# Experts on their own tokens: rows scattered to slots of one expert and gathered back, in a two-layer graph network with a mixture of experts

## The chip, the cores and the metric

The kernel runs on one core of a Trainium2 chip. The core has a matrix engine (PE, with its weight loads shown as PEld), a vector engine (DVE), a scalar engine (ACT), a general engine (POOL, which can also issue DMAs) and a synchronisation engine (SP, which here only issues DMAs). Each engine runs its own instructions in the order in which the built program has them. The metric is the device time of one execution in microseconds, as the median of several runs.

## The reference, cut to what matters

The input is 64 batches of 256 tokens of 256 features, all float32. A dense graph layer, a dense layer, a second graph layer and a mixture of eight experts follow each other, each on the normalised tokens and each added to its input.

```python
x = x + gnn0(layernorm(x), adj, W0, a0)      # 4 heads, softmax over masked scores, elu
x = x + layernorm(x) @ weight.T + bias
x = x + gnn1(layernorm(x), adj, W1, a1)      # 1 head, relu
x = x + moe(layernorm(x))

def moe(tokens):                             # 16384 tokens of 256
    logits = tokens @ router_w.T             # 8 experts
    rw, re = top_k(softmax(logits), 2)
    rw = rw / rw.sum(-1)
    combine = zeros(N, 8).at[arange(N)[:, None], re].set(rw)
    out = tokens
    for e in range(8):
        h = gelu(tokens @ w1[e] + b1[e])
        out = out + combine[:, e:e+1] * (h @ w2[e] + b2[e])
    return out
```

Each token keeps two experts of eight; the loop above computes all eight and weights six of them with zero.

## The kernel before, in words

The kernel is written against a tiling layer: the program is traced in Python, and a scheduler then fixes each engine's order, taking work in the order in which it was traced wherever its inputs and buffers let it. Tiles of one tag rotate through a fixed number of buffers, so an instruction can wait for a buffer as well as for data.

The work goes by pairs of batches: 32 pairs, each of 512 tokens, which are four tiles of 128 rows. `batch_layers` is a generator that does both graph layers and the dense layer for one batch; `layers` lets the two batches of a pair take turns. In one batch, `project` normalises (L159 to L166, with two small POOL operations at L162 and L163), transposes on PE (L176), copies the transposed tokens out of PSUM on ACT (L179) and multiplies with the layer's weights (L190). `attention` makes the scores z per head (L209 to L223), transposes them (L234), copies (L238) and multiplies with q (L241). Four heads in the first graph layer, one in the second. At the end the normalised tokens are transposed into xT (L179 again), and POOL writes base, the sum that the experts add to (L294).

After both batches, `layers` computes the router's logits (L308), ranks the experts and gives weights comb that are zero for six experts (L313 to L334), and adds the second biases (L345, L347).

`experts` then runs each of the eight experts on all 512 tokens of a pair: four products of 512 columns into ph (L357), two gelus (L361), eight products of 256 columns into py (L367) and four weighted additions into base (L373). All expert weights lie on the chip for the whole kernel; POOL loads them at the start (L144 to L150).

The last loop takes one step of the next pair's layers between each two experts of a pair, so the experts of pair p lie beside the layers of pair p+1. SP loads one pair's tokens per step (L66) and stores one pair's result.

Of the kernel before, what the change touches and what calls it, by code (L numbers as in the profile page):

```python
# [8 lines left out]
F32 = mybir.dt.float32  # L9
AF = mybir.ActivationFunctionType  # L10
ALU = mybir.AluOpType
AX = mybir.AxisListType

P = 128


def rows_to_all(ap: bass.AP, n: int) -> bass.AP:
    """A contiguous vector of n elements in DRAM, read into every partition."""
    return bass.AP(tensor=ap.tensor, offset=ap.offset, ap=[[0, P], [1, n]])
# [3 lines left out]
def kernel(  # L23
# [27 lines left out]
    EPS = 1e-5  # L51
    SLOPE0, SLOPE1 = 0.2, 0.01
# [5 lines left out]
    small = ctx.enter_context(tc.tile_pool(name="small", bufs=4))  # L58
    psum = ctx.enter_context(tc.tile_pool(name="psum", bufs=2, space=bass.MemoryType.PSUM))
# [19 lines left out]
    # before[e, f] = 1 where expert f comes before expert e: ties go to the lower index.  # L79
    before = const.tile([P, E, E], F32, tag="before", name="before")  # L80
    nc.vector.memset(before, 0.0)
    for e in range(1, E):
        nc.vector.memset(before[:, e, :e], 1.0)

    adj_i = const.tile([P, NT, N], adj.dtype, tag="adj_i", name="adj_i")
    nc.sync.dma_start(out=adj_i, in_=adj.rearrange("(t p) j -> p t j", p=P))
    # Added to the scores before the leaky ReLU, which brings a masked one to the reference's fill.
# [9 lines left out]
    def gnn_weights(w, a, heads, name):  # L97
        """[W | W a_src | W a_dst], so one product gives q and both score terms."""
# [41 lines left out]
    w1s = const.tile([P, E, KT, D], F32, tag="w1s", name="w1s")  # L140
    w2s = const.tile([P, E, KT, D], F32, tag="w2s", name="w2s")
    b1s = const.tile([P, E, KT], F32, tag="b1s", name="b1s")
    b2s = const.tile([E, D], F32, tag="b2s", name="b2s")
    nc.gpsimd.dma_start(out=b2s, in_=b2)  # L144
    nc.gpsimd.dma_start(out=b1s, in_=b1.rearrange("e (t p) -> p e t", p=P))
    for e in range(0, E, 2):
        nc.gpsimd.dma_start(
            out=w1s[:, e : e + 2], in_=w1[e : e + 2].rearrange("e (k p) f -> p e k f", p=P)
        )
        nc.gpsimd.dma_start(  # L150
            out=w2s[:, e : e + 2], in_=w2[e : e + 2].rearrange("e (k p) f -> p e k f", p=P)
        )

# [1 line left out]
    def layernorm(src):  # L155
# [8 lines left out]
        xn = work.tile([P, NT, D], F32, tag="xn", name="xn")  # L164
# [16 lines left out]
    def project(src, wx, heads):  # L181
        """q of one batch, with both score terms in its last columns."""
# [14 lines left out]
    def attention(q, heads, mask, slope):  # L197
        """Per head: exp(scores - row max), its row sums, and its product with q, in PSUM.

        Yields between the two, and returns the values and 1 / sums.  # L200
        """
# [48 lines left out]
    def batch_layers(p, i, xT, base):  # L250
        """Both graph layers and the dense layer for one batch, in steps."""
# [40 lines left out]
        xn = layernorm(x2)  # L292
        transpose_tokens(xn, xT[:, :, i * N : (i + 1) * N])
        nc.gpsimd.tensor_add(base[:, i * NT : (i + 1) * NT, :], x2, xn)  # L294

    def layers(p):
        """Every layer before the experts for two batches, in steps; the batches take turns."""
        xT = io.tile([P, KT, TOK], F32, tag="xT", name=f"xT_{p}", bufs=3)
        base = io.tile([P, TT, D], F32, tag="base", name=f"base_{p}", bufs=3)
        steps = [batch_layers(p, i, xT, base) for i in range(2)]  # L300
        while steps:
            steps = [g for g in steps if next(g, steps) is not steps]
            yield

        pl = psum.tile([P, TT, E], F32, tag="mm", name="pl")
        for t in range(TT):
            for k in range(KT):
                nc.tensor.matmul(  # L308
                    pl[:, t, :], xT[:, k, t * P : (t + 1) * P], rT[:, k, :],
                    start=(k == 0), stop=(k == KT - 1),  # L310
                )
        lg = small.tile([P, TT, E], F32, tag="lg", name="lg")
        nc.vector.tensor_copy(lg, pl)  # L313
        lmax = small.tile([P, TT], F32, tag="lmax", name="lmax")
        nc.vector.tensor_reduce(lmax, lg, AX.X, ALU.max)
        comb = io.tile([P, TT, E], F32, tag="comb", name=f"comb_{p}", bufs=3)
        nc.vector.tensor_sub(comb, lg, lmax[:, :, None].to_broadcast([P, TT, E]))
        nc.scalar.activation(comb, comb, AF.Exp)
        # How many experts stand ahead of each: a greater logit, or an equal one at a lower index.
        ahead = small.tile([P, TT, E, E], F32, tag="ahead", name="ahead", bufs=1)  # L320
        tie = small.tile([P, TT, E, E], F32, tag="tie", name="tie", bufs=1)
        other = lg[:, :, None, :].to_broadcast([P, TT, E, E])
        own = lg[:, :, :, None].to_broadcast([P, TT, E, E])
        nc.vector.tensor_tensor(ahead, other, own, ALU.is_gt)
        nc.vector.tensor_tensor(tie, other, own, ALU.is_equal)
        nc.vector.tensor_mul(tie, tie, before[:, None, :, :].to_broadcast([P, TT, E, E]))
        nc.vector.tensor_add(ahead, ahead, tie)
        rank = small.tile([P, TT, E], F32, tag="rank", name="rank")
        nc.vector.tensor_reduce(rank, ahead, AX.X, ALU.add)
        nc.vector.scalar_tensor_tensor(comb, rank, 1.5, comb, op0=ALU.is_lt, op1=ALU.mult)  # L330
        tot = small.tile([P, TT], F32, tag="tot", name="tot")
        nc.vector.tensor_reduce(tot, comb, AX.X, ALU.add)
        nc.vector.reciprocal(tot, tot)
        nc.vector.tensor_mul(comb, comb, tot[:, :, None].to_broadcast([P, TT, E]))  # L334

        # The experts' second biases, weighted: comb @ b2.
        pc = psum.tile([E, TT, P], F32, tag="tr", name="pc")
        for t in range(TT):
            nc.tensor.transpose(pc[:, t, :], comb[:, t, :], ident)
        combT = small.tile([E, TT, P], F32, tag="combT", name="combT", bufs=1)  # L340
        nc.vector.tensor_copy(combT, pc)
        for i in range(2):
            pb = psum.tile([P, NT, D], F32, tag="mm", name="pb")
            for t in range(NT):
                nc.tensor.matmul(pb[:, t, :], combT[:, i * NT + t, :], b2s, start=True, stop=True)  # L345
            half = base[:, i * NT : (i + 1) * NT, :]
            nc.vector.tensor_add(half, pb, half)  # L347
        return xT, base, comb

    def experts(p, xT, base, comb):  # L350
        """Every expert on two batches, weighted into base; a step an expert."""
        for e in range(E):
# [82 lines left out]
```

## Time and profile before

| | |
|---|---|
| median of 3 runs | 3353.58 us (3351.46 to 3354.95) |
| span of the profiled execution | 3349.4 us; the page gives no other time for it, so 2 to 6 us of a run lie outside the span |
| instructions | 38810 |
| DVE busy | 1906.8 us (57%) |
| ACT busy | 1695.9 us (51%), of it 436 table loads of 1.283 us |
| POOL busy | 520.8 us (16%) |
| DMA | 41.76 MB, mean 12 GB/s |
| HBM | 22.50 MB read, 16.78 MB written |
| chain of waits, by engine | PE 62%, DVE 22%, ACT 7%, POOL 5%, issue 3% |

The profile page has the busy time of each engine, the span in 40 slices, the chain of work that ended last, and the costliest groups of instructions. A group's row gives its line, engine, operation, tiles and count, then the total busy time, the mean of one instruction in ns, and the engine's idle time just ahead of it with what ended that. The view by windows gives each engine's busy time in a stretch with the clock that PE was granted (PEclk, 1.00 is full), the mean busy share of the 16 DMA engines and the GB/s moved. The view in order of time gives start, duration, engine, line and tiles; rows of SPq are DMA issues on SP.

### The profile page before, as it was taken

The page shows a single profiled execution, that of the slowest core. Times are in us where ns is not written, and L with a number is a line of the kernel's source. Part 1 is how long each engine was busy: PE and PEld are TensorE (multiplying, and loading weights), DVE is VectorE, ACT ScalarE, POOL GpSimd, SP SyncE. Part 2 cuts the span into 40 slices and gives each one's busy share as a digit, 9 for nine tenths or more (in the row PEclk, how much of TensorE's full clock was granted, in tenths as well). Part 3 has the DMA queues.
Part 4 walks back from the last instruction along what each step waited for, and adds up shares of the span by engine and source line. Part 5 has one row for each costly group of instructions (what it writes and reads, how often), then busy time and mean ns, then how long its engine had stood idle before and what let it go on. Part 6 is the DMA issues. An engine that isn't in the chain of part 4 may idle for free.

```text
span 3349.4 us, 38810 instructions
## 1 busy us (share of the span) xinstructions
PE 3101.1 (93%) x14086; PEld 2180.6 (65%) x14086; DVE 1906.8 (57%) x4927; ACT 1695.9 (51%) x3156; POOL 520.8 (16%) x720
## 2 busy tenths in 40 slices
PE   5899999999999999999999999999999999999999
PEld 4566666666666666666666666666666666666666
DVE  5555656556565556565565655565655656555653
ACT  2444555545555445555455554455554555544552
POOL 2111101111111111011111111110111111111100
PEclk7899999999999999999999999999999999999999
DMA  2000000000000000000000000000000000000000
GB/s 88 1 13 13 7 13 13 7 13 13 7 13 7 13 13 7 13 13 7 13 13 7 13 7 13 13 7 13 13 7 13 13 7 13 7 13 13 1 7 13
DMA packets 36750, 41.76 MB, mean 12 GB/s; under 512 B 1344, under 2 KB 35408, under 8 KB 36560
## 3 DMA queue, kind: packets, MB, share of 16 engines
q1 hardware_dynamic: 35328, 35.07, 3.4%
q0 software_dynamic: 1232, 4.21, 0.4%
q8 instruction: 112, 1.84, 0.2%
q14 instruction: 78, 0.64, 0.1%
HBM read 22.50 MB, written 16.78 MB: 12 GB/s over the span
## 4 chain that ended last, share of the span: by engine, by line
PE 62%; DVE 22%; ACT 7%; POOL 5%; issue 3%; DMA 0%; SPq 0%; POOLq 0%; DVEq 0%; ACTq 0%
PE py L367 18%; PE ph L357 12%; PE pv L241 9%; PE pq L190 8%; DVE z L215 5%; PE pt L176 4%; ACT z L223 4%; PE pp L234 3%; DVE z L219 3%; POOL rstd L163 3%; DVE stats L159 3%; DVE xn L166 3%; DVE nmax L221 2%; PE pd L209 2%; PE pb L345 2%
## 5 line engine op out<-in xcount | busy, mean ns | idle before, releaser
L367 PE MATMUL py<-w2s,hT 128*128 128x256 f32 x4096 | 1046.0, 388 | 39.5 <-ACT hT L361 26.5
L357 PE MATMUL ph<-xT,w1s 128*128 128x512 f32 x2048 | 1003.4, 603 | 14.8 <-ACT hT L361 14.8
L367 PEld LDWEIGHTS py<-w2s,hT 128*128 128x128 f32 x4096 | 739.2, 191 | 264.2 <-issue 81.1
L373 DVE SCALAR_TENSOR_TENSOR base<-py,comb,base 128x256 f32<-128x256 f32 x1024 | 458.1, 473 | 401.5 <-PE py L367 401.5
L361 ACT ACTIVATE hT<-ph,b1s 128x512 f32<-128x512 f32 x512 | 349.3, 688 | 491.1 <-PE ph L357 486.3
L357 PEld LDWEIGHTS ph<-xT,w1s 128*128 128x128 f32 x2048 | 370.6, 192 | 231.0 <-issue 190.4
L215 DVE SCALAR_TENSOR_TENSOR z<-pd,q,mask 128x256 f32<-128x256 f32 x640 | 285.7, 475 | 301.1 <-PE pd L209 301.1
L241 PE MATMUL pv<-q,zT 128*128 128x64 f32 (+1 forms) x2560 | 385.1, 301 | 20.5 <-ACT zT L238 20.5
L162 POOL TENSOR_SCALAR rstd<-mv 128x2 f32<-128x2 f32 x256 | 61.3, 239 | 2194.3 <-DVE mv L160 2125.4
L241 PEld LDWEIGHTS pv<-q,zT 128*128 128x128 f32 x2560 | 343.1, 194 | 71.7 <-ACT zT L238 57.7
L179 ACT COPY xnT<-pt 128x512 f32<-128x512 f32 x192 | 109.1, 584 | 493.2 <-PE pt L176 493.2
L223 ACT ACTIVATE z<-z,nmax 128x256 f32<-128x256 f32 x640 | 317.9, 497 | 48.4 <-DVE nmax L221 47.3
L361 ACT ACT_TABLE_LOAD x218 | 279.7, 1283 | 84.5 <-PE ph L357 81.2
L176 PE MATMUL pt<-ident,xn 128*128 128x128 f32 x1024 | 170.1, 290 | 131.3 <-DVE xn L166 128.7
L176 PEld LDWEIGHTS pt<-ident,xn 128*128 128x128 f32 x1024 | 113.3, 143 | 266.7 <-issue 204.4
L190 PE MATMUL pq<-wx,xnT 128*128 128x258 f32 (+1 forms) x1024 | 268.4, 415 | 1.4 <-ACT xnT L179 1.4
L190 PEld LDWEIGHTS pq<-wx,xnT 128*128 128x128 f32 x1024 | 214.4, 210 | 78.1 <-ACT xnT L179 28.6
L166 DVE TENSOR_SCALAR xn<-x,mv,rstd 128x256 f32<-128x256 f32 x384 | 140.8, 409 | 158.2 <-POOL rstd L163 158.2
L238 ACT COPY zT<-pp 128x512 f32<-128x512 f32 x320 | 174.6, 585 | 91.2 <-PE pp L234 91.0
L219 DVE SCALAR_TENSOR_TENSOR z<-z 128x512 f32<-128x512 f32 x320 | 217.7, 680 | 1.1
L221 DVE TENSOR_REDUCE nmax<-z 128x2 f32<-128x512 f32 x320 | 215.9, 675 | 1.1
L223 ACT ACT_TABLE_LOAD x155 | 198.9, 1283 | 2.8
(72 smaller groups left out, 2695.6 us busy)
## 6 DMA issues: line engine op xcount, KB each, us to landing
xin<-in_x_dram SPq DMA_DIRECT2D x32, 512.0 KB, 3.7
out_dram<-base SPq DMA_DIRECT2D x32, 512.0 KB, 2.9
w1s<-in_L_ffn_w_dram POOLq DMA_DIRECT2D x4, 512.0 KB, 12.2
w2s<-in_L_ffn_w_dram POOLq DMA_DIRECT2D x4, 512.0 KB, 13.0
wx<-in_L_gnn_W_dram SPq DMA_DIRECT2D x2, 256.0 KB, 5.0
adj_i<-in_adj_dram SPq DMA_DIRECT2D x1, 256.0 KB, 4.3
wx_a<-in_L_gnn_a_dram SPq DMA_DIRECT2D x1, 256.0 KB, 7.0
wf_in<-in_L_ffn_weight_dram SPq DMA_DIRECT2D x1, 256.0 KB, 9.9
```

The lines of the kernel that those rows point to most:

```text
L166: nc.vector.tensor_scalar(xn[:, t, :], src[:, t, :], mv[:, t, 0:1], rstd[:, t : t + 1], op0=ALU.subtract, op1=ALU.mult,)
L176: nc.tensor.transpose(pt[:, k, t * P : (t + 1) * P], xn[:, t, k * P : (k + 1) * P], ident)
L190: nc.tensor.matmul(pq, xnT[:, k, t * P : (t + 1) * P], wx[:, k, :], start=(k == 0), stop=(k == KT - 1),)
L215: nc.vector.scalar_tensor_tensor(z[:, t, :], pd, q[:, t, c_src : c_src + 1], mask[:, t, :], op0=ALU.add, op1=ALU.add,)
L219: nc.vector.scalar_tensor_tensor(z, z, slope, z, op0=ALU.mult, op1=ALU.max)
L221: nc.vector.tensor_reduce(nmax, z, AX.X, ALU.max, negate=True)
L223: nc.scalar.activation(z[:, t, :], z[:, t, :], AF.Exp, bias=nmax[:, t : t + 1], accum_out=sums[:, t, h : h + 1],)
L241: nc.tensor.matmul(pv[:, t, h * d : (h + 1) * d], zT[:, j, t * P : (t + 1) * P], q[:, j, h * d : (h + 1) * d], start=(j == 0), stop=(j == ...
L357: nc.tensor.matmul(ph, w1s[:, e, k, f * P : (f + 1) * P], xT[:, k, :], start=(k == 0), stop=(k == KT - 1),)
L361: nc.scalar.activation(hT[:, f, :], ph, AF.Gelu, bias=b1s[:, e, f : f + 1])
L367: nc.tensor.matmul(py[:, s, :], hT[:, f, t * P : (t + 1) * P], w2s[:, e, f, :], start=(f == 0), stop=(f == KT - 1),)
L373: nc.vector.scalar_tensor_tensor(base[:, t, :], py[:, s, :], comb[:, t, e : e + 1], base[:, t, :], op0=ALU.mult, op1=ALU.add,)
```

## The change: what it does

The experts run only on the tokens that keep them.

- **Groups.** The 32 pairs are cut in groups of 9, 9, 8 and 6 pairs. For each group the normalised tokens stay on chip, the logits of all its tokens are collected, and base goes to DRAM per batch.
- **Dispatch.** Once a group's layers are done, `dispatch` finds each token's two experts and weights and numbers its rows, expert after expert, so that every expert's rows start at a multiple of 128. A group of nt tiles gets 2 nt + 7 slots of 128 rows: 79, 79, 71 and 55 slots, 284 in all.
- **Send.** POOL scatters each tile of 128 rows twice into a DRAM buffer xs by an indirect DMA (L459).
- **Slot.** For each slot SP reads the expert's number from SBUF into a register (L475), fetches that expert's weights and biases (128 rows of 1282 floats, four buffers, L477) and the slot's rows (L480). PE transposes the rows (L483), DVE copies them, PE multiplies (L489), ACT does two gelus (L495), PE multiplies (L500), DVE adds the bias, and SP stores the rows to ys (L506).
- **Combine.** Per tile, SP loads base (L511), POOL gathers the two rows of each token (L514), DVE weights and adds (L518), and SP stores the result (L521).
- **Order.** The sends, slots and combines of group g are traced between the steps of group g+1's layers, spread over its steps. The first group's layers have nothing beside them, and the last group's sends, slots and combines come after all layers.
- **Start.** The expert weights are packed into DRAM and both xs buffers are filled with zeros, through DMAs issued by ACT.

The routing on comb, the resident expert weights and the loop `experts` go away.

```diff
+    wpack = tc.dram_tile([E, P, WROW], F32, name="wpack")
+    for e in range(E):
+        wt = io.tile([P, WROW], F32, tag="we", name=f"wt_{e}", bufs=4)
...
+        nc.scalar.dma_start(out=wpack[e], in_=wt)
+    zero = const.tile([P, 2, D], F32, tag="zero", name="zero")
...
+        for s in range(0, SLOTS, 2):
+            n = min(2, SLOTS - s)
+            nc.scalar.dma_start(
+                out=xs[s * P : (s + n) * P, :].rearrange("(t p) d -> p t d", p=P),
+                in_=zero[:, :n, :],
+            )
...
-        xn = layernorm(x2)
-        transpose_tokens(xn, xT[:, :, i * N : (i + 1) * N])
-        nc.gpsimd.tensor_add(base[:, i * NT : (i + 1) * NT, :], x2, xn)
+        xn = layernorm(x2, keep, "xng", 2 * max(GROUPS) + 4)
+        xng.append(xn)
+        xnT = work.tile([P, KT, N], F32, tag="xnT", name="xnT")
+        transpose_tokens(xn, xnT)
+        pl = psum.tile([P, NT, E], F32, tag="mm", name="pl")
...
+        nc.vector.tensor_copy(lg, pl)
+        nc.gpsimd.tensor_add(x2, x2, xn)
+        nc.sync.dma_start(
+            out=base_d[g][r0 * P : (r0 + NT) * P, :].rearrange("(t p) d -> p t d", p=P), in_=x2
+        )
...
+    def send(g, t, xn, pos):
+        for k in range(2):
+            d = nc.gpsimd.indirect_dma_start(
+                out=xs_d[g % 2][:, :],
+                out_offset=bass.IndirectOffsetOnAxis(ap=pos[k][:, t : t + 1], axis=0),
+                in_=xn, in_offset=None,
+            )
...
+    def slot(g, j, ei):
+        with tc.issue_after(fetched[-1]) if fetched else nullcontext():
+            e = nc.sync.value_load(ei[0:1, j : j + 1], min_val=0, max_val=E - 1)
+        we = io.tile([P, WROW], F32, tag="we", name="we", bufs=4)
+        fetch = nc.sync.dma_start(out=we, in_=wpack[bass.ds(e, 1), :, :].rearrange("e p c -> (e p) c"))
+        fetched.append(fetch.ins)
+        xr = io.tile([P, D], F32, tag="xr", name="xr", bufs=4)
+        nc.sync.dma_start(out=xr, in_=xs_d[g % 2][j * P : (j + 1) * P, :])
+        px = psum.tile([P, KT, P], F32, tag="px", name="px", bufs=1)
+        for k in range(KT):
+            nc.tensor.transpose(px[:, k, :], xr[:, k * P : (k + 1) * P], ident)
+        xT = work.tile([P, KT, P], F32, tag="xT", name="xT")
+        nc.vector.tensor_copy(xT, px)
+        ph = psum.tile([P, KT, P], F32, tag="ph", name="ph", bufs=2)
+        for f in range(KT):
+            for k in range(KT):
+                nc.tensor.matmul(
+                    ph[:, f, :], we[:, k * D + f * P : k * D + (f + 1) * P], xT[:, k, :],
+                    start=(k == 0), stop=(k == KT - 1),
+                )
+        hT = work.tile([P, KT, P], F32, tag="hT", name="hT", bufs=3)
+        for f in range(KT):
+            nc.scalar.activation(
+                hT[:, f, :], ph[:, f, :], AF.Gelu, bias=we[:, C_B1 + f : C_B1 + f + 1]
+            )
+        py = psum.tile([P, D], F32, tag="py", name="py", bufs=1)
...
+        y = io.tile([P, D], F32, tag="y", name="y", bufs=4)
+        nc.vector.tensor_add(y, py, we[:, C_B2:])
+        nc.sync.dma_start(out=ys_d[g % 2][j * P : (j + 1) * P, :], in_=y)
+
+    def combine(g, row0, t, pos, wts):
+        o = io.tile([P, D], F32, tag="o", name="o", bufs=6)
+        nc.sync.dma_start(out=o, in_=base_d[g][t * P : (t + 1) * P, :])
+        for k in range(2):
+            yk = io.tile([P, D], F32, tag=f"yk{k}", name=f"yk{k}", bufs=6)
+            nc.gpsimd.indirect_dma_start(
+                out=yk, out_offset=None, in_=ys_d[g % 2][:, :],
+                in_offset=bass.IndirectOffsetOnAxis(ap=pos[k][:, t : t + 1], axis=0),
+            )
+            nc.vector.scalar_tensor_tensor(
+                o, yk, wts[k][:, t : t + 1], o, op0=ALU.mult, op1=ALU.add
+            )
+        nc.sync.dma_start(out=out_rows[row0 + t * P : row0 + (t + 1) * P, :], in_=o)
...
+            for _ in layers(p, g, q * TT, xng, lg):
+                n = -(-left // max(steps_left, 1))
+                steps_left -= 1
+                for _ in range(n):
+                    next(behind, None)
+                left -= n
+            p += 1
+        for _ in behind:
+            pass
+        routed = dispatch(g, nt, lg)
+        behind = background(g, row0, nt, xng, routed)
+        left = 4 * nt + E - 1
+    for _ in behind:
+        pass
```

## The prediction

> **What bounds the kernel now.** I read the groups by cost first, then the windows, then the rows in order of time.
>
> ```profile
> PE 3101.1 (93%) x14086; PEld 2180.6 (65%) x14086; DVE 1906.8 (57%) x4927; ACT 1695.9 (51%) x3156; POOL 520.8 (16%) x720
> ...
> L367 PE MATMUL py<-w2s,hT 128*128 128x256 f32 x4096 | 1046.0, 388 | 39.5 <-ACT hT L361 26.5
> L357 PE MATMUL ph<-xT,w1s 128*128 128x512 f32 x2048 | 1003.4, 603 | 14.8 <-ACT hT L361 14.8
> ```
>
> PE is busy 93% of the span, and 2049.4 of its 3101.1 us are the two expert products. That leaves 1052 us of PE for the layers, 33 us for each of 32 pairs. If the layers were limited by PE too, taking three quarters of the experts away would be a large gain. So the question is what a pair's layers cost with little or nothing beside them. The first pair of this trace shows it, since no experts are ready yet. Its normalised tokens begin to be written at 18.12 us, those of the second pair at 108.42:
>
> ```profile
> 18.12 1.54 DVE L166 TENSOR_SCALAR xn<-xin,mv,rstd 128x256 f32<-128x256 f32 x4 [1.01 <-POOL rstd L163]
> ...
> 108.42 0.73 DVE L166 TENSOR_SCALAR xn<-xin,mv,rstd 128x256 f32<-128x256 f32 x2 [1.57 <-POOL rstd L163]
> ```
>
> So a bare pair takes 90.3 us, not 33. The same stretch by windows:
>
> ```profile
> 18.00:40.00 22.00, 11.36 (x44) 7.76 (x44) 16.06 (x34) 9.82 (x31) 0.90 (x2) 0.75 0.23 79
> 40.00:58.00 18.00, 17.94 (x91) 17.16 (x92) 5.76 (x15) 6.60 (x17) 2.19 (x3) 0.55 0.00 1
> 58.00:86.00 28.00, 15.98 (x57) 11.84 (x57) 10.98 (x29) 5.57 (x13) 4.01 (x7) 0.77 0.06 19
> 86.00:108.00 22.00, 10.64 (x42) 8.09 (x40) 8.85 (x27) 3.44 (x8) 7.42 (x10) 0.73 0.00 1
> ```
>
> After the stretch and its length come busy times of PE, PEld, DVE, ACT, POOL, then PE's clock. No engine is full throughout: DVE leads, then PE at a clock of 0.55, then a chain of hand-offs. Now a pair in the middle of the run, with eight experts beside it:
>
> ```profile
> 1556.07 1.08 ACT L179 COPY xnT<-pt 128x512 f32<-128x512 f32 x2 [7.47 <-PE pt L176]
> ...
> 1642.46 0.59 ACT L179 COPY xT<-pt 128x512 f32<-128x512 f32 x1
> ...
> 1656.99 1.08 ACT L179 COPY xnT<-pt 128x512 f32<-128x512 f32 x2 [5.79 <-PE pt L176]
> ```
>
> From first to last transposed copy its layers take 86.4 us; the first pair took 19.80 to 107.00, 87.2. A pair's whole period is 100.9 us. The layers are a chain of about 87 us whether 2049.4/32 = 64 us of expert products stand in it or none. What fewer products can win is mainly the 12 us between 88 and 101, in 32 pairs; against that stand a first group and a tail that lie beside nothing.
>
> **The change part by part.** The built program's order shows per pair what stands where. Pairs are counted from 0.
>
> *Removed.* PE loses 2049.4 us and gains 284 slots of two transposes, four products of 128 columns and two of 256. At the rows' 290 and 388 ns a slot is 6 x 0.290 + 2 x 0.388 = 2.5 us, so 714 us. ACT's table loads fall from 436 to 174, by 336 us. DVE loses the 458.1 us of L373 and the routing, and gains two operations a slot and two a tile, some 0.45 us each. By the 87 us above, none of it is worth its size.
>
> *Start.* ACT's order holds 119 DMAs before its first copy, which is now at 19.80 us and which every pair waits for. They move 8 x 524 KB = 4.2 MB of weights and 8 x 131 KB = 1.0 MB of second biases in, 8 x 656 KB = 5.3 MB of packs out and 158 x 131 KB = 20.7 MB of zeros out; with SP's first loads about 33 MB.
>
> ```profile
> 0.00:20.00 20.00, 2.78 (x13) 2.25 (x14) 11.51 (x43) 1.48 (x2) 10.66 (x20) 1.00 0.92 288
> ```
>
> At this 288 GB/s it is 115 us; eight transfers may still be under way when ACT goes on, so its first copy comes near 112. Bounds: 119 issues of 0.45 us alone (54 us), or half the rate (230 us). I take +92 us: the first pair begins at 110.
>
> *Group 0.* Nine pairs with no slot in PE's order, built like the bare first pair. The next pair's transposes now stand behind the logits of the second batch, so the period goes from 18.68 (first L176) to 109.5 (L308 from 107.64, 1.88 long): 9 x 90.8 = 817, to 927 us. I know no reason for less, since the clock of 0.55 to 0.77 comes with this density.
>
> *The other 23 pairs.* PE's order has 229 slots in them: 5, 10, 11, 17, 15, 15, 6, 0, 0 in group 1, 5, 10, 11, 19, 20, 14, 0, 0 in group 2, and 6, 13, 25, 20, 7, 0 in group 3. A pair then has 10 slots on average: 25 us of PE against 64 now, ten times two gelus of some 0.4 us (L361's 0.688 is for four times the columns), 7 to 8 table loads against 13.6. That is less inserted work than the middle pair above carried, so its 86.4 us hold, plus 2 for logits and the next transposes: 88.5 x 23 = 2036 us. Bounds: 76, the chain with PE always at full clock (worked out under the rivals), and 101, today's period.
>
> *Dispatch.* Some 23 operations of 288 columns at about 0.45 us and a dozen small ones at 0.2: 13 to 15 us on DVE, of which the next pair's first wait for PE (5.74 us in the first pair) hides a part. 10 us each for three groups: 30.
>
> *Sends.* No row has an indirect DMA. The nearest are POOL's own issues:
>
> ```profile
> 1.30 0.72 POOL L144 DMA_DIRECT2D b2s<-in_L_ffn_b_dram  x1 [0.36 <-issue]
> ...
> 2.38 1.24 POOL L145 DMA_DIRECT2D b1s<-in_L_ffn_b_dram  x1
> ```
>
> Lower end 0.72; upper end 1.5, POOL's 512 KB loads landing after 12.2 us with eight under way (12.2/8). I take 1.2, near the issue with most pieces. POOL's order has 46 sends ahead of the second layernorm of the pair after a dispatch: 55 us, where the chain needs it 36 us after its start (54.31 less 18.12). 19 us late, for three groups 57 (0 to 99). Behind those two POOL operations waits the whole pair; the first slot waits for all 72 sends.
>
> *Gathers.* 208 in these pairs. A layernorm's POOL operations stand behind half an issue, 0.6 us, eight times a pair, in about 8 pairs: 38 us (0 to 60). Their stores and loads on SP cost issues of 0.45 us beside other work.
>
> *Tail.* After the last pair nothing covers the last group: dispatch 15; 48 sends at 1.2, 58; landing and first fetch 10; 55 slots; 48 gathers, 58; last store 3. In PE's order each tail slot ends before the next begins: transposes 0.5, copy 0.45, products 0.85, two gelus 0.8, products 0.6, four hand-offs of 0.1: 3.6 us, 198 for 55. Beside it the slot's 919 KB take 3.2 us at 288 GB/s, and SP needs three issues of 0.45 and the register read. That read has no row: between one issue (0.43) and a landing of 8 KB (4.4); I take 1.0, nearer SP's own rows, and SP is then at 2.4. Sum 342; with 4.4 SP sets 5.8 us a slot, 461.
>
> The Trainium skill, "DMA: Bandwidth & Descriptors", section "Latency and other measured facts", gives a tensor load a floor of about 0.6 us; no row here shows it, and by it SP would be at 2.0 us a slot and the tail stay 342.
>
> *Sum.* 110 + 817 + 2036 + 30 + 57 + 38 + 342 = 3430 us of span against 3349.4. Medians lie 4 us above the span: **3434 us**, 2.4% slower.
>
> **The rivals.**
>
> *PE warms up and the chain shortens (faster).* In the middle pair eight L190 products of the second layer take 1.91 us, in the first pair 3.81. At full clock the chain loses 3.8 there, 1.8 in the last L241, 0.9 each in the first L190 and L308, and of the 18 us at 0.55 some 6: 13 to 14 us. If slots keep the clock above 0.95 without standing in the way, the 18 pairs that have slots take 76: 3434 - 18 x 12.5 = 3209, and with sends at 0.72 it is 3152. For it: windows with experts show a clock of 1.00. Against it: at 40 to 58 us PE was 17.94 of 18 us busy and still at 0.55, and the middle pair at 1.00 needed 86.4. It turns faster if these pairs fall below 84.
>
> The Trainium skill, "TensorE: Matmul & The Clock Gate", section "Why this matters for your kernels", asks for no PE gap above about 3 us between bursts, else half clock; that speaks against bare pairs, whose gaps reach 5.8 us, and for this rival where slots fill them, which would make 3209. The row of 0.55 without a gap shows that gaps are not all of it.
>
> *Slots come late (much slower).* PE, DVE and ACT run in a fixed order, so a slot whose weights have not landed stops the layers behind it. A fetch lands after 4.7 us (512 KB in 3.7, scaled) or, as POOL's weights did, 15.6 (12.2 scaled). With four buffers and 4 us of computing a slot then needs 2.2 or 4.9 us. From a landing of about 10 us it exceeds the 3.6 of the order; at 15.6 I put 1.3 us on each of 284 slots: 3434 + 369 = 3800. Plain bandwidth does not do it: even the pair with 25 slots moves 23 MB, 80 us at 288 GB/s.
>
> *It saves less than it says.* Padding makes 284 slots, not 256, whatever the tokens do; those 28 are in the sum (7 of them in the tail, 25 us).
>
> **How the numbers follow.** Forecast case, 3360 to 3600: 0.46. Late slots, above 3600: 0.20. Warm chain, below 3347: 0.31. Within 0.2%, about what a measurement of this kernel can tell from no change: 0.03. So faster 0.31, slower 0.66. Leaving out 0.08 of the warm case and 0.11 of the late one, the range is 3190 to 3800; the likeliest case alone is 3360 to 3600.
>
> **What would show it.** Right: nothing but DMAs on ACT until about 112 us; pairs 0 to 8 each near 91 us at a clock of 0.55 to 0.8; the last layer's end near 3090, then some 340 us with PE under half busy. Wrong: a bare group at under 85 us a pair, pairs with slots below 84 or above 100, an indirect DMA far from 1.2 us on POOL, tail slots far from 3.6 us.

## The result, and the profile after

The changed kernel takes **3905.26 us** (median of 4 runs, 3899.14 to 3914.45) against 3354.26 us (4 runs, 3351.46 to 3356.39): a ratio of 1.1644, 95% interval 1.1627 to 1.1662. It is slower, as forecast, but by 551 us, not by 80; the time lies above the range. The profiled execution has a span of 3904.8 us, 475 above the 3430 of the prediction's sum. At another time the same program took 3980 us (last part of the experiments), so each experiment is compared with the run of the changed kernel whose profile looks alike: 3909.69 us (condition I) or 3980.34 us (condition II, with waits in the profile that nothing in it explains).

Four lines of the page of the changed kernel: its busy times, TensorE's clock in 40 slices, and the two groups of indirect DMAs on POOL.

```profile
PE 2493.0 (64%) x11550; PEld 2016.8 (52%) x11550; DVE 1750.3 (45%) x4484; ACT 1196.2 (31%) x2922; POOL 998.8 (26%) x1227
...
PEclk9666666666578888866658899956668997555555
...
L514 POOL DMA_INDIRECT yk<-ys,pos x256 | 255.4, 998 | 444.1 <-DMA ys<-y 345.2
...
L459 POOL DMA_INDIRECT xs<-xng,pos x256 | 249.1, 973 | 144.2 <-issue 72.7
```

PE lost 608 us of work and the span still grew by 555. No engine is above 64%. The clock row falls to 0.6 in the first quarter, to 0.5 and 0.6 again around the first three dispatches, and to 0.5 in the tail. The windows of the changed kernel show the same by stage (stretch, length, busy time of PE, PEld, DVE, ACT and POOL, PE's clock, DMA share, GB/s): group 0; the first pair after a dispatch; two pairs with ten or eleven slots each; the tail's first slots; the rest of the tail's slots.

```profile
115.00:882.00 767.00, 504.12 (x1885) 399.89 (x1885) 345.66 (x864) 199.17 (x543) 124.50 (x176) 0.61 0.04 12
988.00:1126.00 138.00, 67.50 (x294) 54.31 (x294) 49.03 (x129) 30.81 (x78) 85.17 (x94) 0.64 0.36 126
1126.00:1301.00 175.00, 139.62 (x767) 115.64 (x766) 98.49 (x257) 92.78 (x202) 29.93 (x44) 0.85 0.36 116
...
3540.00:3565.00 25.00, 19.51 (x99) 15.75 (x100) 6.13 (x15) 4.37 (x14) 0.00 (x0) 0.84 0.61 190
3565.00:3830.00 265.00, 216.66 (x666) 162.04 (x666) 39.88 (x94) 29.35 (x94) 0.00 (x0) 0.50 0.50 161
```

Read from one first copy of `q` to that of the next pair (ACT's L241 in the timeline), the periods are:

| pairs (counted from 0) | what stands beside the layers | period, us |
|---|---|---|
| 1 to 7 | nothing | 95.2 to 95.9 |
| 9, 18, 26 | 72, 72 and 64 sends, a few slots | 138.5, 138.6, 130.2 |
| 10, 11, 19, 20, 27 | 10 to 12 slots | 86.9, 88.4, 86.9, 86.0, 90.4 |
| 12 to 14, 21, 22, 28, 29 | 15 to 26 slots | 98.7 to 112.8 |
| 15, 23, 30 | 6 to 16 slots, then the first gathers | 135.1, 123.2, 145.9 |
| 16, 17, 24, 25 | the other gathers (17 and 25 with 10 us of dispatch) | 101.8, 105.3, 106.8, 103.5 |

The layers end at 3460 us, where 3088 was forecast, and the tail takes 445 us instead of 342. Two things strike the eye. Ten slots make a pair shorter than no slots. And every row of the table with indirect DMAs is long. How the sends come to cost 43 us is seen in POOL's and VectorE's timeline of pair 9 (start, duration, engine and line, idle time before and what ended it):

```profile
1047.51 0.96 POOL L459 DMA_INDIRECT xs<-xng,pos  x1 [0.30 <-issue]
1048.78 0.96 POOL L459 DMA_INDIRECT xs<-xng,pos  x1 [0.30 <-issue]
...
1052.30 0.24 POOL L209 TENSOR_SCALAR rstd<-mv 128x2 f32<-128x2 f32 x1
...
1054.53 0.79 DVE L213 TENSOR_SCALAR xn<-x,mv,rstd 128x256 f32<-128x256 f32 x2 [25.32 <-POOL rstd L210]
```

An indirect DMA is busy 0.96 us, and the next starts 1.26 us after it. The second layernorm's POOL operation stands behind 46 of them; VectorE has nothing else to do and waits 25 us. In pair 8, without sends, this operation came 34.1 us after the pair's first copy of `q`; here it comes 64.8 us after it.

### The profile page after: what moved, and what is told of

Same layout as the page of the kernel before. It is cut to its first block, busy times and chain, and to the rows that moved or that the text cites. A ratio compares the mean times of both kernels' runs of the same rounds, so it can differ in the third digit from the quotient of the medians.

```text
span 3904.8 us, 38293 instructions
## 1 busy us (share of the span) xinstructions
PE 2493.0 (64%) x11550; PEld 2016.8 (52%) x11550; DVE 1750.3 (45%) x4484; ACT 1196.2 (31%) x2922; POOL 998.8 (26%) x1227
## 5 line engine op out<-in xcount | busy, mean ns | idle before, releaser
L288 PE MATMUL pv<-q,zT 128*128 128x64 f32 (+1 forms) x2560 | 555.7, 385 | 43.2 <-ACT zT L285 42.6
L489 PE MATMUL ph<-xT,we 128*128 128x128 f32 x2272 | 386.0, 316 | 74.7 <-DVE xT L485 72.6
L489 PEld LDWEIGHTS ph<-xT,we 128*128 128x128 f32 x2272 | 347.4, 223 | 120.8 <-DVE xT L485 110.3
L500 PE MATMUL py<-we,hT 128*128 128x256 f32 x1136 | 372.4, 449 | 58.0 <-ACT hT L495 48.7
L514 POOL DMA_INDIRECT yk<-ys,pos x256 | 255.4, 998 | 444.1 <-DMA ys<-y 345.2
L495 ACT ACTIVATE hT<-ph,we 128x128 f32<-128x128 f32 x568 | 179.5, 365 | 587.1 <-issue 414.6
L281 PE MATMUL pp<-ident,z 128*128 128x128 f32 x1280 | 294.2, 376 | 37.8 <-DVE z L262 35.5
L459 POOL DMA_INDIRECT xs<-xng,pos x256 | 249.1, 973 | 144.2 <-issue 72.7
L500 PEld LDWEIGHTS py<-we,hT 128*128 128x128 f32 x1136 | 220.2, 217 | 118.6 <-ACT hT L495 85.2
L281 PEld LDWEIGHTS pp<-ident,z 128*128 128x128 f32 x1280 | 237.9, 213 | 55.2 <-issue 32.3
```

Of the source, the lines that this page charges most:

```text
L281: nc.tensor.transpose(pp[:, j, t * P : (t + 1) * P], z[:, t, j * P : (j + 1) * P], ident)
L288: nc.tensor.matmul(pv[:, t, h * d : (h + 1) * d], zT[:, j, t * P : (t + 1) * P], q[:, j, h * d : (h + 1) * d], start=(j == 0), stop=(j == ...
L459: d = nc.gpsimd.indirect_dma_start(out=xs_d[g % 2][:, :], out_offset=bass.IndirectOffsetOnAxis(ap=pos[k][:, t : t + 1], axis=0), in_=xn, i ...
L489: nc.tensor.matmul(ph[:, f, :], we[:, k * D + f * P : k * D + (f + 1) * P], xT[:, k, :], start=(k == 0), stop=(k == KT - 1),)
L495: nc.scalar.activation(hT[:, f, :], ph[:, f, :], AF.Gelu, bias=we[:, C_B1 + f : C_B1 + f + 1])
L500: nc.tensor.matmul(py, hT[:, f, :], we[:, C_W2 + f * D : C_W2 + (f + 1) * D], start=(f == 0), stop=(f == KT - 1),)
```

## The experiments

**Theory A** after this reading: what was not foreseen is POOL's clumps of indirect DMAs ahead of the layernorm, and a cold TensorE clock where no slots stand beside the layers (group 0, and the tail). **Rival B**, from the prediction: slots come late, because their weights have not landed, and stop the layers behind them. Theories C and D come up on the way.

**1. The order on POOL** (condition II).

```
+            with tc.issue_after(pows[-1]):       # last layernorm power traced
                 d = nc.gpsimd.indirect_dma_start(...)   # sends; the gathers alike
```

> Only the order on POOL is changed: each send and gather is queued behind the last layernorm power operation of the layer step beside which it is traced, so at most 16 indirect DMAs stand in a row where 44 did. Theory A (POOL's clumps and a cold TensorE clock make the 471 us that were not foreseen): the three pairs after a dispatch fall from 138.5, 138.6 and 130.2 us to about 102, the three pairs with the first gathers from 135.1, 123.2 and 145.9 to about 108, in all some 190 us, so 3715 us. Rival B (slots come late: a slot whose rows or weights have not landed stops the layers behind it): POOL's order does not matter, the time stays within 20 us of 3905.

Measured 3970.42 us, 10 below 3980.34, which is no difference. Against the changed kernel under the like condition, the first pairs after a dispatch fell from 152.6, 152.6 and 145.4 to 121.7, 121.5 and 129.4 us, but the second pairs rose from 87.2, 87.3 and 91.3 to 106.6, 106.6 and 108.2 and the third from 87.0 and 89.3 to 104 (in the last group it fell). Spread out, the 72 sends took 195 us instead of 110, and the slots behind them moved: TensorE's order has 0, 4 and 20 slots in pairs 9 to 11, where it had 4, 10 and 11. Over the three pairs the time is 332 us against 327. Of the gathers, 36 moved behind the last pair's first copy, and that pair's layers took 113 us instead of 91. Theory A's form "clumps" falls: what the layernorm no longer waits for is paid by cold pairs without slots, by crowded ones and by the last pair. The comparison even flatters this kernel: its profile has 37 us of the unexplained waits (experiment 11), that of the 3980.34 us has 243, and against 3909.69 us, where there are none, it is 61 us slower.

**2. Weights held in SBUF** (condition II).

```
-        e = nc.sync.value_load(ei[0:1, j : j + 1], ...)
-        we = io.tile([P, WROW], F32, tag="we", ...); nc.sync.dma_start(out=we, in_=wpack[...])
+        we = we0          # expert 0, loaded once
```

> Leaves out: every slot uses the weights of expert 0, held in SBUF from the start, so there is no register read and no fetch (182 MB less). Theory A: fetches are not what holds the layers, so the time stays near 3890, with tail slots still near 5.6 us at a TensorE clock of 0.5 and pairs with 15 to 20 slots still near 100 us. Rival B: the twelve pairs with slots and without gathers fall from 96 us in the mean to 88 (95 us in all) and the tail slots from 5.6 to 3.6 us (110), so about 3700.

Measured 3807.17 us, 173 less. The pairs stay: 152.4 with sends, 100.8, 99.0 and 99.0 with 15 to 17 slots, so rival B does not hold for the weights beside the layers (the slots' rows are still fetched here). Of the gain, 148 us are in the tail, where a slot takes 2.5 us. That was not in theory A's number, and rival B was right there by its sign. Two rows of TensorE in the tail of the changed kernel, and two in this one:

```profile
3744.21 2.08 PE L489 MATMUL ph<-xT,we 128*128 128x128 f32 x8 [0.52 <-DVE xT L485]
...
3746.79 2.07 PE L500 MATMUL py<-we,hT 128*128 128x256 f32 x4 [0.51 <-ACT hT L495]
```

```profile
3652.40 1.05 PE L486 MATMUL ph<-xT,we 128*128 128x128 f32 x8
...
3653.97 1.13 PE L497 MATMUL py<-we,hT 128*128 128x256 f32 x4 [0.30 <-ACT hT L492]
```

The same products take 4.15 us at a clock of 0.50 and 2.18 at 0.98. Without fetches the program's order is another one too: the next slot's transposes stand ahead of a slot's second products, as they do in the first seven slots of the changed kernel, of which the third to the sixth also take 2.5 to 2.6 us each. From the eighth on they stand behind, so a slot is one chain. So this run does not separate the fetch from the order; experiments 4 and 8 do.

**3. Idle slots in group 0** (condition II).

```
+                if g == 0:
+                    for _ in range(2):      # each of five steps of a pair
+                        idle_slot()         # constant rows and weights, result dropped
```

> Adds work: in each of the nine pairs of group 0, ten slots that need no data from the dispatch (constant rows and weights, no DMA, the result is dropped). Theory A: bare pairs take 95.5 us because TensorE runs at a clock of 0.6; with ten slots they run at about 0.85 and take 87, as the pairs with ten real slots do, so group 0 gets about 70 us shorter with 90 slots more: 3835 us. The account by inserted work (2.2 us a slot, the difference between pairs with 17 and with 10 slots): 200 us longer, 4100.

Measured 3903.53 us: 77 less than 3980.34, with 90 slots of work more. Pairs 1 to 7 take 84.8 to 87.8 us instead of 95.5. One window, group 0 of this kernel:

```profile
121.00:810.00 689.00, 547.09 (x3051) 450.46 (x3050) 396.74 (x1031) 370.06 (x807) 120.24 (x176) 0.86 0.05 14
```

The clock is 0.86 where it was 0.61. So the cold clock costs a bare pair 10 us, and ten slots are hidden in it.

**4. The tail's slots interleaved** (condition II).

```
-        slot(g, j, ei)
+        A(j + 2); B(j + 1); C(j)   # A: loads, transposes; B: first products; C: second products, store
+        # B's products queued behind A's transposes, C's behind B's; last group only; five weight buffers
```

> Only the tail's slots are changed: in TensorE's order the transposes of slot j+2, the first products of j+1 and the second products of j stand together, so that no hand-off to another engine lies between them; five weight buffers in place of four. Theory A (5.60 us a slot is one chain at half clock, 2.08 and 2.07 us of products that take 1.05 and 1.13 at full clock): TensorE has no gaps left, goes to full clock, and a slot takes 2.6 to 3.2 us (the latter is its 919 KB at 288 GB/s); tail 130 to 160 us shorter, about 3760. Rival B (fetch, register read and in-order queue of SP set the slot): stays at 5.6 us a slot, 3905.

Measured 3856.49 us, 124 less, of which 108 are in the tail; a slot takes 3.3 us. Window of the tail's slots of this kernel:

```profile
3600.00:3775.00 175.00, 115.03 (x725) 94.72 (x725) 42.77 (x103) 32.55 (x104) 0.00 (x0) 0.97 0.83 263
```

The clock is 0.97, and now transfers set the pace: 263 GB/s at a DMA share of 0.83, and of the 60 us that TensorE is idle in this window all but 0.3 end with the landing of a slot's rows. The serial order at half clock was worth 2.3 us of the 5.6, nearly all of it the clock's, as experiment 8 shows.

**5. The floor** (condition I).

```
-        routed = dispatch(g, nt, lg)
-        behind = background(g, row0, nt, xng, routed)
```

> Leaves out the whole expert part: no dispatch, sends, slots or gathers; the start with its fills and all layers stay. Theory A: 32 bare pairs at 95.5 us behind a start of 115: 3170 us, with a clock of 0.61 throughout. It is the floor of this change in this order of the layers: about 180 us under the kernel before, out of which every send, slot and gather of 284 slots has to be paid.

Measured 3175.31 us. The layers from the first pair on:

```profile
119.00:3081.00 2962.00, 1948.80 (x7313) 1547.37 (x7312) 1341.73 (x3348) 772.91 (x2107) 484.73 (x682) 0.61 0.04 11
```

Each pair takes 95.6 us at a clock of 0.61. A kernel that computes no experts at all in this order is 5% faster than the kernel before. That is all the change could have gained without the start and the clock being changed too.

**6. No indirect DMAs** (condition I).

```
-            d = nc.gpsimd.indirect_dma_start(out=xs_d[g % 2][:, :], out_offset=..., in_=xn, ...)
+            nc.sync.dma_start(out=xs_d[g % 2][j * P : (j + 1) * P, :], in_=xn)   # j = 2 t + k; gathers alike
```

> Leaves out: the permutation. Each send and each gather is one plain 128 KB transfer on the SP queue, with the same number of transfers and bytes (so slots hold other rows and the output is not the reference's). Takes away all indirect DMAs at once, with POOL's time, their packets and whatever else they disturb. Theory A and C both: the six pairs with many indirect DMAs fall from 811 us together to about 600, the later gather pairs by some 30 us, and the tail by 96 x (1.26 - 0.45) = 78 us: near 3600. The difference to the run with POOL freed is what indirect DMAs cost beside POOL's time.

Measured 3578.22 us, 331 less. The six pairs fall from 811 us to 588 (the order now has 11 slots in the first pair after a dispatch), the other gather pairs to about 95, the tail by 99. So **with plain transfers of the same size in place of the 512 indirect DMAs the kernel is 331 us shorter**: 237 in the pairs from 9 to 30 and 99 in the tail, less 5 that group 0 is longer. Not all of this is the DMAs' own: the slots stand in other places, and in the tail some 20 us come from slots that run longer at full clock (the clock stays at 1.00 for 44 us there, for 14 in the run of 3909.69 us).

**7. POOL freed** (condition I).

```
-        nc.gpsimd.tensor_scalar_add(rstd, mv[:, :, 1], EPS)
-        nc.gpsimd.tensor_tensor(rstd, rstd, mhalf, ALU.pow)
+        # nine VectorE operations: a bit estimate and two Newton steps; the three additions on VectorE too
```

> All work of the layers leaves POOL: the layernorm's inverse root is computed on VectorE (a bit estimate and two Newton steps, nine small operations), and the three additions of a batch too. POOL only issues indirect DMAs. Theory A, second form (every indirect DMA, 1.26 us from one to the next, is inserted ahead of POOL operations of the chain, wherever it stands; 40 to 45 us for 72 of them): the pairs with sends fall from 138.5 to about 100, those with gathers from 101 to 146 to about 95; about 230 us less in all, near 3680. Theory C (while POOL issues a row of indirect DMAs, TensorE's own instructions come late, as the waits without releaser suggest): these pairs keep most of their 120 to 145 us, near 3850.

Measured 3999.30 us, 90 more than 3909.69. Both theories fail in their numbers. Bare pairs rise to 94 to 103 us, the price of the VectorE operations. The first pairs after a dispatch still take 142.8, 142.8 and 137.1. TensorE's row shows why (POOL's last send started at 1125.92):

```profile
1130.53 0.69 PE L491 MATMUL px<-ident,xr 128*128 128x128 f32 x2 [40.44 <-DMA xr<-xs]
```

The layers now run past the sends undisturbed until TensorE meets the first slot in its fixed order. It waits 40 us for the last send to land. Freed from one queue, the sends' 91 us are met at the next. With the gathers it is the same: from pair 15's first gather to its last, VectorE's weighted sums, mixed with the layers' operations in its order, wait for one gather after the other (37 us in all), and pair 15 takes 142.6 us. This gives **theory D**: indirect DMAs cost what the first thing behind them in an engine's fixed order has to wait, and the planner that made the order put those things too early.

**8. The later start** (condition II, two runs).

```
-        nc.scalar.dma_start(...)   # packs and zero fills ahead of ACT's first copy
+        nc.sync.dma_start(...)     # two packs and ten fills beside each pair of group 0
```

> Only the start is changed: packing the expert weights (40 DMAs) and filling the slot rows with zeros (78 DMAs) are issued by SP during the nine pairs of group 0 instead of by ACT ahead of its first copy. All theories: the first pair begins near 25 us instead of 115, the pairs of group 0 stay at 95.5 us since nothing there waits for DMAs; 85 to 90 us less, near 3820.

> The later start again. Without the waits that have no shown releaser: 3905 less the 90 us of the start, near 3815. With them, 3879 again.

Measured 3878.75 and 3864.61 us, 102 and 116 below 3980.34. The first copy of `q` comes at 19.9 us instead of 118.5, and group 0 keeps its 95.5 us a pair: 99 us of the gain.

The tail of the second run is 24 us shorter, and its trace shows why. TensorE's order is that of the changed kernel, a slot as one chain, but for the twelve slots from 3541 us on the clock is 1.00. They take 3.6 us each where nothing is waited for; once the clock has fallen to 0.50, the slots after them take 5.6. Two rows of one of them, two windows, and the row with which the fall begins:

```profile
3545.51 1.16 PE L487 MATMUL ph<-xT,we 128*128 128x128 f32 x8 [0.63 <-DVE xT L483]
3547.17 1.13 PE L498 MATMUL py<-we,hT 128*128 128x256 f32 x4 [0.51 <-ACT hT L493]
...
3541.00:3582.00 41.00, 27.89 (x154) 20.57 (x155) 8.41 (x22) 6.89 (x22) 0.00 (x0) 1.00 0.78 245
3597.00:3780.00 183.00, 149.73 (x459) 112.08 (x460) 27.23 (x64) 20.74 (x66) 0.00 (x0) 0.50 0.52 163
...
3590.86 0.41 PE L481 MATMUL px<-ident,xr 128*128 128x128 f32 x2 [1.22 <-DMA xr<-xs]
```

So of a tail slot's 5.6 us the clock alone is 2.0, and the interleaved order of experiment 4 takes off another 0.3. The products slow down right behind a wait of 1.22 us for a slot's rows here, and of 1.41 us in the changed kernel (at 3563.73); whether that wait is the cause is not shown.

**9. Later consumers** (condition II, three runs).

```
+            [sends(g), steps 0 to 4], [slots(g), step 5 to the last; the first pinned behind the layers' transposes],
+            [combines(g - 1), steps 5 to 14; weighted sums one step behind their gathers]
+        on_dve[0] = g > 0 and q < (3 if g > 1 else 2)    # these pairs keep the layers off POOL
```

> The consumers of the indirect DMAs are put later, and POOL is freed where they run: in the first pair after a dispatch only the sends run beside the layers, the slots begin in the pair after it (pinned in TensorE's order), the gathers of a group run one group later, beside slots, and VectorE's weighted sums stand one layer step behind their gathers; in these pairs (two or three of a group) the layernorm's inverse root and the additions are on VectorE. Theory D (72 indirect DMAs take 91 us wherever they are; what they cost is the wait of the first thing behind them in the fixed order of an engine, which the order's planner puts too early: POOL's layernorm, TensorE's first slot, VectorE's weighted sum): the 138 us pairs fall to about 100, the 135 us pairs to about 95, in all about 300 us less, near 3600. If indirect DMAs disturb the layers in themselves, the pairs beside them stay above 115 us: above 3750.

> The later consumers again. Without the waits that have no shown releaser, theory D says near 3600, with first pairs after a dispatch near 100 us. With them, 3969 again, with first pairs of 178 to 198 us.

> The later consumers a third time, since both runs so far had 515 us of waits for TensorE without a shown releaser, and the unchanged kernel shows that such waits come and go with the chip or the moment (none in two of its profiles, 243 us in the third, at 75 us more). Where they are absent, theory D says near 3600. Where they are there, 3969 again, and theory D cannot be decided.

Measured 3969.35, 3969.74 and 3971.26 us (the last with 1.1833 of the time before, interval 1.1799 to 1.1868). The pairs of pure slots are the best of all: five pairs in a row with ten slots each took 86.2 and then 85.2 to 85.3 us. Three of them, by window:

```profile
1436.00:1692.00 256.00, 202.35 (x1130) 166.64 (x1129) 148.18 (x384) 138.34 (x301) 44.98 (x66) 0.86 0.39 121
```

But the first pairs after a dispatch took 177 to 198 us: pair 9, with nothing beside the layers but its 72 sends, 177 to 179, and pairs 18 and 26, which had got 16 gathers as well, 184 to 198. Theory D is not confirmed; condition II makes this reading unsafe, as the next runs show.

**10. The whole set, without and with idle slots** (condition II).

```
+    GROUPS = (5, 8, 8, 7, 4)     # with the later start, the interleaved tail, the later consumers
+    if g == 0 or q == 0: two idle slots a step       # second kernel only
```

> The later consumers, the start's DMAs in group 0, the tail's slots in three interleaved parts, and groups of 5, 8, 8, 7 and 4 pairs. By the terms found so far: start 25, five bare pairs 478, five dispatches 50, four pairs with sends 400, 23 pairs at 93 us 2139, tail 243 (40 sends and 32 gathers at 1.26, 39 slots at 3.4 us, 15 for the dispatch): 3335 us, about as the kernel before. If theory D is wrong, above 3500.

> The run before with work added: ten idle slots (constant rows and weights, no DMA, result dropped) in each pair of group 0 and in each pair with sends, nine pairs that else have no products of the experts. If the cold clock sets the bare pairs, they fall by 9 to 10 us each, as in the first experiment of this kind: about 85 us below the run without them, near 3250 and so below the kernel before. If they only add work: 90 x 2.2 = 200 us above it.

> The whole set with idle slots again. Without the waits that have no shown releaser, near 3250. With them, 3668 again.

> The whole set with idle slots a third time. Where the waits without releaser are absent, near 3250, below the kernel before. Where they are there, 3660 again.

Measured 3752.97 us without, and 3667.66, 3659.52 and 3665.40 us with idle slots: 85 us less for 90 slots more, as forecast. The totals are some 415 above the expectation. In the run without idle slots, 286 of it are the four pairs with sends (131 to 191 us each, where 100 were counted; three of them also hold 18 gathers), and 75 the tail, in which 88 gathers stand instead of 32. The best version is 315 us below the changed kernel under the like condition, and still 1.0922 (1.089 to 1.0954) of the kernel before. No version tried beats the kernel before.

**11. The changed kernel itself**, once beside experiments 5 to 7, and once beside the first repetitions of 8 to 10. The other runs have none beside them; what puts them under condition II is their profiles.

> The changed kernel again, unchanged. In three of the four experiments so far, in the pairs whose POOL issues indirect DMAs, waits for TensorE's products of 4 to 45 us ended without a releaser that the profile shows, 87 to 130 us in all, and the first pair after a dispatch took 152 to 155 us instead of 138.5; the profile of the changed kernel shows none. If these waits differ from execution to execution, they may appear here too, with the same total near 3905 us; if they come from the edits, the first pair after a dispatch is 138.5 us again.

> The changed kernel once more, beside three kernels that showed waits for TensorE without a shown releaser, all on one chip. If these waits belong to the chip or the moment, all four of this call have them or none (then this one takes 3905 or about 3960 together with the others' gain or loss). If they belong to the program, this one has none and the three others have them again: 3905, 3879, 3969, 3668.

Measured 3909.69 and 3980.34 us. The same program, 71 us apart, 60 of it in the pairs with indirect DMAs (pair 9: 138.48 and 152.59) and 8 in the first pair. In the second profile, four rows of pair 9 while POOL sends:

```profile
1015.10 1.27 PE L281 MATMUL pp<-ident,z 128*128 128x128 f32 x5
1023.55 0.59 ACT L285 COPY zT<-pp 128x512 f32<-128x512 f32 x1 [9.27 <-remote]
...
1025.95 1.70 PE L281 MATMUL pp<-ident,z 128*128 128x128 f32 x7
1048.06 0.59 ACT L285 COPY zT<-pp 128x512 f32<-128x512 f32 x1 [22.93 <-remote]
```

ACT waits 9 and 23 us for transposes that TensorE's rows show as long done (at 1016.38 and 1027.65), and the view names no instruction that ended the wait ("remote"). The trace does have a step of TensorE's semaphore, the counter by which it tells others that it is done, at 1023.53 and 1048.04; all 19 such waits of this profile end with a step of it that comes late, or is recorded late. Such waits add up to 243 us here, to 37 to 270 in experiments 1 to 4 and 8, and to 325 to 591 in experiments 9 and 10 (waits of several engines for one cause are counted each), to none in any run of condition I. They stand where indirect DMAs run, or just behind. The profiles of condition II also lack records: of the steps that tell of landings this one has 21,937, that of condition I for the same program 29,493, and no transfer's landing can be told from it. Whether that is one cause, and what it is (the chip, its host, or how it is profiled), these runs do not tell; when it was run decided, not the program. So theory D is left open: no run of the later consumers fell under condition I.

## Why the prediction was right and wrong, point by point

The 475 us between the forecast span and the measured one, by the prediction's terms:

| step of the prediction | forecast | measured | missing |
|---|---|---|---|
| start, ACT's first copy | 112 | 112.12 | 0 |
| group 0, nine pairs (dispatch apart) | 817 | 863 | 46 |
| pairs 9 to 30, layers and slots (by experiment 6) | 1947 | 2129 | 182 |
| sends and gathers in them (the difference to experiment 6) | 95 | 237 | 142 |
| tail | 342 | 445 | 103 |

The rows add up to 473. Row three is the 2149 us of experiment 6 less 20 us for two dispatches.

- **Direction and start: right,** though the likeliest case, 3360 to 3600, was far too low. The start's 115 us at 288 GB/s were ACT's 112, and experiment 8 takes 99 of them away.
- **"The other 23 pairs", 88.5 us each: the step that failed most.** It took inserted work below that of the kernel before as free. Its ground, 86.4 us for the layers of the middle pair against 87.2 for the bare one, was an agreement by chance: the one had a clock of 1.00 and 64 us of products between, the other a clock of 0.71 and none. (Its period of 100.9 us is also one of three such; 27 of the 31 periods of that kernel are 102.5 or 102.6.) With plain transfers the pairs average 96.8 us. At ten slots the assumption was better than right (85 to 87 us). It is wrong on both sides of that: a pair without slots is cold, 95.5 us, and the order puts 15 to 26 slots into others, where the ones above ten cost 1.3 to 2.5 us each (pair 12: 101.9 less 87.6 us, over 6.5 slots, is 2.2). The counts per pair stood in the prediction; an average of ten was made of them, and the cost is not linear.
- **Group 0: mis-sized by 5 us a pair.** The one bare pair of the kernel before ran at a mean clock of 0.71 (its four windows, weighted by length); the steady bare pair runs at 0.61.
- **Sends, 57 us: right mechanism, size off.** The queue and the place were named: 46 sends ahead of the second layernorm. They end 31 us late, not 19: sends begin 6.6 us after the pair's first copy, behind the dispatch on VectorE, and go on at 1.26 us. The other 26 sends, counted as harmless, stand ahead of the next layernorms, and the second batch's third one comes 44 us late. Experiment 6 gives 131 us for the three pairs (138.48, 138.75 and 130.73 less 92.65, 94.06 and 90.08).
- **Gathers, 38 us: the order was not read.** They were costed as spread evenly, half an issue ahead of each layernorm. POOL's order has them in rows of 8 to 19. The pairs with gathers and the rest pay about 106 us for it (237 less 131), of which pairs 15, 23 and 30 pay 93.
- **1.2 us for an indirect DMA: right** (1.26 from one to the next), in part by luck: it was taken near one plain issue of 1.24 us, while here 0.96 us are busy and 0.30 a gap.
- **Tail, 3.6 us a slot: mis-sized by the clock.** That a slot ends before the next begins was right. The products were put at 1.45 us. They take 2.2 to 2.3 at full clock (a product has two rows in the trace, so that L489 has 2272 for 284 slots of four, and the prediction counted one) and 4.15 at half clock. At full clock the chain does take 3.6 us, as experiment 8 shows, but by luck: the gelus and hand-offs, put at 1.0 us between the products, leave TensorE idle for 0.5. 55 slots took 294 us, not 198. SP's register read, which made the bound of 461, was not what set it.
- **Rivals.** "Slots come late" gave the nearest time (3800) by the wrong cause: experiment 2 shows that the fetches of weights do not hold the layers. What did come late once POOL was freed is a slot's rows, 40 us behind the sends (experiment 7). The warm chain was real and is worth 10 us a pair (experiment 3), but only with about ten slots in every pair, which the order gives to few.

The Trainium skill, "TensorE: Matmul & The Clock Gate", section "HAM oscillation — how this bites in real kernels", has as the abstract rule for a warm TensorE "no PE-idle gaps >~3.4µs." The tail disagrees: its gaps are 0.5 us, PE is busy 217 of 265 us, and the clock is 0.50 throughout; where it fell, no gap was above 1.41 us.

## What to carry to other kernels

When work is taken off a full engine, ask first what the rest takes alone, at the clock it will then have: here the layers alone took 95% of the old time. Price a row of indirect DMAs (1.26 us for 128 rows) at the first thing behind it in each engine's fixed order (25 us at a layernorm, 40 us at a slot here), read that order pair by pair, and don't average over it; that putting this first thing later wins the time back is not shown. Work that fills gaps of TensorE can be free or better; a chain that leaves them can run at half clock, and its durations must then be taken from such a row.

## What the runs showed of the hardware that was not expected

- Adding ten slots of work to a bare pair makes it 10 us shorter (95.5 to 85.2; clock 0.61 to 0.86).
- TensorE stays at half clock at 82% busy with gaps of 0.5 us (tail), and at 0.98 at 88% busy with gaps of 0.3 us (experiment 2). But the tail's chain also ran at 1.00 for twelve slots, 68% busy and with gaps of 0.5 to 0.85 us (second run of experiment 8), so neither figure gives the clock by itself.
- An indirect DMA of 128 rows of 1 KB holds POOL for 0.97 us, and the next one starts 0.30 us later, for scatter and gather alike; 72 take 91 us.
- The same program can run 71 us apart at two times, with waits of up to 44 us for TensorE's semaphore, during indirect DMAs, long after its rows have ended; the cause is open.
